# Normalising and turning one attention operand closer to its use, and a reordered first attention, in a two-layer fp32 attention kernel

## The chip, the cores and the metric

The kernel runs on one core of a Trainium2 chip. The metric is device time in microseconds (us). Three runs of the kernel before took 230.91, 231.04 and 232.44 us; the median is 231.04 us.

A core has five engines that follow queues of their own: TensorE (PE, matrix products and transposes, with a separate queue of weight loads, PEld), VectorE (DVE), ScalarE (ACT), GpSimd (POOL) and SyncE (SP, which here only issues transfers). They wait for each other by semaphores.

## The reference

There are two inputs, `x` and `ctx` (called c in the kernel), each 32 batches of 256 tokens by 256 features, fp32. Two layers follow each other.

```python
# L0: attention of x on ctx with 16 heads of 16 features
q, k, v = heads(x @ Wq.T), heads(ctx @ Wk.T), heads(ctx @ Wv.T)
att = softmax(q @ k.T / 4) @ v
x = x + att[0]                # batch 0's result is added to every batch

# L1
nX = layernorm(ctx) * norm1_w + norm1_b
nF = layernorm(x)   * norm2_w + norm2_b
attended = softmax(nF @ nX.T / 16) @ nX                   # each batch by itself
h = gelu(attended @ fc1_w.T + fc1_b)                      # 4 features
cross = h @ fc2_w.T + fc2_b
nC = layernorm(cross) * norm3_w + norm3_b
own = softmax(nC @ nC.T / 16) @ nC
out = nF + gamma2 * (cross + gamma1 * own)
```

Because only `att[0]` is used, L0 is worked out for batch 0 alone. Because `h` has four features, everything behind `attended` is done in a space of five to nine columns.

## The kernel before, in words

**Layout.** Batches go in quads (`QB = 4`, `NQ = 8` quads). The 256 tokens of a batch lie in two halves of 128 partitions. c has four rotating quad buffers, `cq`; x lies whole in `x_all`. Both are normalised in place, without the weights of the norm, which are folded into later operations.

**Order.** The program is written out by hand: the order of the calls is the order of the instructions in each engine's queue, and only the semaphores between engines are put in by the framework. So an instruction that waits holds up all that the code issues later on the same engine.

**The heads of L0** (L670 to L736). The 16 heads go in four groups of four. For each group, `head_queries` makes scores on PE, from which `head_maxima` takes the row maxima on DVE; `head_less` turns the maxima and subtracts them; `head_keys` makes the scores once more, the other way round, with ACT taking the exponential; `head_values` weighs the values with them, and `head_turned` turns the result into a part of `att`, which is complete after the fourth group. `project_values` makes the values that `head_values` needs. Between these calls stand the first steps for c: `stats(n)` (DVE, two `bn_stats` per batch), `moments_c` (POOL), `even_normed` (POOL normalises a batch's first 128 tokens) and `odd_normed` (ACT normalises the other 128). The small set-ups of weights (`setup_bias` and others) are spread among them.

**Between the heads and the steps** (L831 to L849) `add_attention` starts to add `att` to x: a transfer issued by POOL that adds `att`, broadcast over four batches (1 MB), into `x_all`. The first batches of x get it from DVE instead, by `add_first`.

**The loop** calls `first_step(s)` (L869) for s = 0, 1, ... A step makes the scores of batch s (`cross_scores`: eight matmuls `sc`, L779), then the maximum of each row (`nm`, DVE, L789), and the exponential (`e`, ACT, L792). Two steps later `cross_turned` turns the exponentials (PE, `pt_e`) and ACT copies them (`eTq`). By quad, `values` and `values_turned` make the reduced values of c, `cross_values` and `cross_weighted` the weighted sums. What makes later batches ready stands ahead of the scores in a step:

- `load_c(q)` and `load_x` are issued by SP. A load of c waits until its buffer is free, which is when the last batch of the quad four earlier has been turned and used.
- `stats_c` and `stats_x` put the statistics of a batch (`st`, DVE, L211) into tiles of a quad.
- `moments` (L213 to L241, on POOL unless another engine is given) turns the statistics of 8 or 16 columns into a factor `rs` and a shift `nmr`; it holds a power, `rs` from `ve` (L227). `moments_both(q)` does it in one block of 16 columns for the x of quad q and the c of quad q + 1, `moments_c` and `moments_x` for one alone.
- `norm_c` normalises both halves of a batch of c on POOL (L307). `norm_x` has POOL do one half (L329) and ACT the other (L331).
- `turn_c` turns a normalised batch of c (four transposes on PE, `pt_c`), which DVE or ACT copies to `nxT`; `turn_x` does the same for x with ACT (`nfT`, L761).
- Eight memsets (`zeroed`), six of them 128 x 1024, fill on POOL, in steps 8 to 15, tiles that the second part needs.

In the kernel before, in the steady part of the loop, step s takes the statistics of batch s + 12 of c, normalises batch s + 8 and turns batch s + 4. x keeps a distance of 8, 4 and 1. The last step of a quad calls the moments after its statistics:

```python
        if b == QB - 1 and 4 <= q + 2 < NQ:
            if q + 3 < NQ:
                moments_both(q + 2)
            else:
                moments_x(q + 2, 0, QB)
        if QB < s < B - 1:
            turn_x(s + 1)
```

After the loop the second part (the layer norm of `cross`, the attention of `nC` on itself, the output) follows in a written order; the change leaves it as it is.

Of the kernel before, what the change touches and what calls it, by code (L numbers as in the profile page):

```python
# [17 lines left out]
NC = D // P  # L18
# [4 lines left out]
QB = 4  # L23
# [4 lines left out]
def tile_xattn_seq(  # L28
# [179 lines left out]
    def statistics(st, src):  # L208

        for t in range(NC):  # L210
            nc.vector.bn_stats(st[:, t, :], src[:, t, :])  # L211

    def moments(st, n, name, eng=None):  # L213

        eng = eng or nc.gpsimd

        def t(what, c=1, bufs=2):
            return small.tile([P, n, c], F32, tag=f"{what}{n}", name=f"{what}_{name}", bufs=bufs)

        sm, df, sq, v4, ve, nm = t("sm", 2), t("df"), t("sq"), t("v4"), t("ve"), t("nmean")  # L220
        rs, nmr = t("rs", 1, 3), t("nmr", 1, 3)
        eng.tensor_sub(df, st[:, :, 1:2], st[:, :, 4:5])
# [4 lines left out]
        nc.gpsimd.tensor_tensor(  # L227
            rs.rearrange("p n o -> p (n o)"),
            ve.rearrange("p n o -> p (n o)"),
            neg_half[:, 0:n],  # L230
            ALU.pow,
        )

        def product():
            eng.tensor_scalar(nm, sm[:, :, 0:1], -0.5, 0.0, ALU.mult, ALU.add)
            eng.tensor_mul(nmr, nm, rs)  # L236
# [10 lines left out]
    def st_tile(q):  # L247

        if q not in st_of:
            st_of[q] = small.tile([P, 2, QB, NC, 6], F32, tag="st", name=f"st_{q}", bufs=5)  # L250
        return st_of[q]

    def stats_c(n):
        q, b = n // QB, n % QB
        statistics(st_tile(q - 1)[:, 0, b], cq_of[q][:, b])

    def stats_x(n):
        q, b = n // QB, n % QB
# [2 lines left out]
    def flat(st):  # L261
        return st.rearrange("p b t c -> p (b t) c")

    def moments_c(q):
        rn = moments(flat(st_of[q - 1][:, 0]), TQ, f"c{q}")
        for b in range(QB):
            mc_of[q * QB + b] = *rn, b * NC

    def moments_ahead(q):

        rs, nmr, product = moments(flat(st_of[q - 1][:, 0]), TQ, f"c{q}", nc.vector)
        for b in range(QB):
            mc_of[q * QB + b] = rs, nmr, b * NC
        return product

    def moments_x(q, lo, hi):
        rn = moments(flat(st_of[q][:, 1, lo:hi]), (hi - lo) * NC, f"x{q}_{lo}")
# [18 lines left out]
    def moments_both(q):  # L296

        rn = moments(st_of[q].rearrange("p k b t c -> p (k b t) c"), 2 * TQ, f"b{q}")
        for b in range(QB):
            mc_of[(q + 1) * QB + b] = *rn, b * NC  # L300
            mx_of[q * QB + b] = *rn, TQ + b * NC

    def norm_c(n):
# [361 lines left out]
    def stats(*ns):  # L665
        for n in ns:
            stats_c(n)
# [15 lines left out]
    less()  # L683
    head_maxima(1, sq, (1, 2, 3))
    setup_fc1()
    project_values(0, on_scalar)
    head_keys(0)
    setup_queries()
    stats(2)
    head_less(1)()  # L690
    setup_outer()
    stats(3)
    project_values(1, on_scalar)
    moments_c(0)
    even_normed(0, 1, 2, 3)
    sq = head_queries(2)
    stats(4)
    head_maxima(2, sq, (0, 1))
    head_values(0)
    setup_bias()  # L700
    head_maxima(2, sq, (2, 3))
    head_keys(1)
    odd_normed(0, 1)
    weighted = head_turned(0)
    stats(5)
    head_less(2)()
    weighted()
    sq = head_queries(3)
    stats(6)
    head_maxima(3, sq, range(QB))  # L710
    head_values(1)
    odd_normed(2, 3)
    head_keys(2)
    weighted = head_turned(1)
    stats(7)
    moments_c(1)
    even_normed(4, 5)
    head_less(3)()
    weighted()
    head_keys(3)  # L720
    stats(8, 9, 10)
    head_values(2, by_vector)
    stats(11)
    odd_normed(4)
    head_values(3, on_scalar, True)
    c_ends = moments_ahead(2)
    weighted = head_turned(2), head_turned(3)
    for f in weighted:
        f()
# [115 lines left out]
    ends()  # L845
    stats_x(2)
    ends = first_moments(2, 3)
    c_ends()
# [13 lines left out]
    ]  # L862


    scaled_at = [25, 26, 26, 27, 27, 28, 29, 29, 31, 31, 32, 32]

    first_ends = [ends]

    def first_step(s, between=()):  # L869
        q, b = s // QB, s % QB  # L870
        if b == 0 and 2 <= q and q + 4 < NQ:
            load_c(q + 4)
            if q == 2:
                load_x((NQ - 2) * QB, B)
        if s in (2, QB):
            add_attention((s // 2 + 2) * QB, (s // 2 + 3) * QB)
        elif b == 0 and 1 < q < NQ - 3:
            add_attention((q + 3) * QB, (q + 4) * QB)

        late_turn = s in (27, 29, 31)  # L880
        if 0 <= s - 2 < B and not late_turn:
            cross_turned(s - 2)
        if 2 <= s < 2 * QB:
            for n in (2 * s, 2 * s + 1):
                stats_x(n)
            if s < QB:
                ends = first_moments(2 * s, 2 * s + 2)
        if QB <= s and s + 3 * QB < B:
            stats_c(s + 3 * QB)
        if s >= 2 * QB and s + 2 * QB < B:  # L890
            stats_x(s + 2 * QB)
        if b == QB - 1 and 4 <= q + 2 < NQ:
            if q + 3 < NQ:
                moments_both(q + 2)
            else:
                moments_x(q + 2, 0, QB)
        if QB < s < B - 1:
            turn_x(s + 1)
        for n in {9: (12,), 10: (13, 14), 11: (15,)}.get(s, ()):
            norm_x(n)  # L900
        if 3 * QB <= s < B - 2 * QB:
            norm_x(s + QB)
        elif B - 2 * QB < s <= B - QB:
            norm_x(s + QB - 1)
        if s + QB < B and s >= QB:
            turn_c(s + QB, on_scalar if s < QB + 2 else by_vector)
        for n in {7: (13,), 8: (14, 15), 9: (16, 17), 10: (18,)}.get(s, ()):
            norm_c(n)
        if 2 * QB + 2 < s < B - 2 * QB:
            norm_c(s + 2 * QB)  # L910
        for n, at in enumerate(scaled_at):
            if s == at:
                scale_skip(n)
        if 2 * QB <= s < 2 * QB + len(zeroed):
            nc.gpsimd.memset(*zeroed[s - 2 * QB])
        if b == 2 and 1 < q < NQ:
            values_turned(q)
        if b == 1 and 1 < q < NQ:
            values(q)
        if b == 2 and 0 < q <= NQ:  # L920
            cross_values(q - 1)
        if b == 3 and 0 < q <= NQ:
            cross_weighted(q - 1)
        for f, *args in between:
            f(*args)
        if s < B:
            softmax = cross_scores(s)
            if s <= QB:
                turn_x(s + 1)
            if s == 0:  # L930
                turn_c(6, nc.scalar.copy)
            softmax()
        if late_turn:
            cross_turned(s - 2)
        if 1 <= s <= QB:
            stats_c(s + 3 * QB - 1)
        if s == 0:
            first_ends.pop()()
            add_first(3)
            first_ends.append(first_moments(3, QB))  # L940
            odd_normed(7)
        elif s == 1:
            first_ends.pop()()
            odd_normed(8)
            even_normed(8, 9)
        elif s == 2:
            ends()
            turn_c(7)
            load_c(5)
            odd_normed(9)  # L950
            even_normed(10)
        elif s == 3:
            ends()
            values(1)
            even_normed(11)
        elif s == QB:
            values_turned(1)
        if s in (QB, QB + 1):
            odd_normed(s + 6)
        if s == QB:  # L960
            moments_x(2, 0, 2)
        elif s == QB + 1:
            norm_x(2 * QB)
# [12 lines left out]
    n_flat = n_all.rearrange("p g t b c -> p (g t b) c")  # L976
# [373 lines left out]
```

## Time and profile before

| what | value |
|---|---|
| median of three runs | 231.04 us |
| the profiled execution | 231.46 us |
| its span in the trace | 229.7 us |
| mean granted clock of TensorE | 0.978 |
| PE busy | 210.5 us, 92 % of the span |
| DVE busy | 171.3 us, 75 % |
| ACT busy | 146.7 us, 64 % |
| POOL busy | 173.8 us, 76 % |
| transfers, mean rate | 147 GB/s |

The span is the time between the first and the last instruction of the trace, and the profiled execution's own time is 1.8 us longer. A share of the span is a mean over stages: the stages have different limits, so a change in one is read from the busy times and the waits of that stage. In the lines of the trace an entry such as `cq<-cq,rs_b,nmr_b 128x256` means output, inputs and shape; the first number of a timeline's line is the time in us since the start of the span, the second the duration, and `x2` means that the line stands for two instructions in a row. A line of the waits names the waiting instruction and line, behind the arrow what ended the wait, then the total, the number and the longest of these waits in us.

### The profile page before, as it was taken

What the parts mean: (1) busy time and instruction counts of PE and PEld (TensorE: products, weight loads), DVE (VectorE), ACT (ScalarE), POOL (GpSimd) and SP (SyncE); (2) the same over time, 40 slices, a digit from 0 to 9 for tenths busy, and PEclk for the clock granted to TensorE, in tenths of its full rate; (3) what the DMA queues carried; (4) which work ended last, traced back from release to release, by engine and by line L of the source; (5) the groups of instructions that cost most, each with busy time, mean ns of one, the idle gap of its engine ahead of it and who ended that gap; (6) DMA issues with size and microseconds to landing.
All of it is one profiled execution on the core that took longest, in us unless ns stands there. A gap on an engine that the chain in (4) does not pass through costs nothing.

```text
span 229.7 us, 4945 instructions
## 1 busy us (share of the span) xinstructions
PE 210.5 (92%) x1797; PEld 153.1 (67%) x1797; DVE 171.3 (75%) x408; ACT 146.7 (64%) x302; POOL 173.8 (76%) x274
## 2 busy tenths in 40 slices
PE   7999898898999989999999999989998979999950
PEld 6766555676787768697897887866675544665530
DVE  2797989899988748667686786777284994796991
ACT  2554968688988285966789967447847735636310
POOL 6067588576989999999979899996089999994000
PEclk9999999999999999999999999999999997999995
DMA  7899997999959974190730000000000002444596
GB/s 224 280 345 344 394 380 152 198 244 246 207 100 335 279 122 172 31 155 2 129 56 1 3 0 0 3 3 4 4 0 3 0 0 107 182 173 182 195 382 251
DMA packets 18038, 33.81 MB, mean 147 GB/s; under 512 B 1175, under 2 KB 2142, under 8 KB 18014
## 3 DMA queue, kind: packets, MB, share of 16 engines
q1 hardware_dynamic: 12974, 24.33, 30.1%
q0 software_dynamic: 3696, 7.34, 18.3%
q10 hardware_dynamic: 1344, 1.84, 2.3%
q8 instruction: 14, 0.23, 0.4%
q14 instruction: 10, 0.08, 0.1%
HBM read 17.73 MB, written 8.39 MB: 114 GB/s over the span
## 4 chain that ended last, share of the span: by engine, by line
PE 59%; DVE 15%; POOL 15%; ACT 6%; issue 3%; DVEq 1%; POOLq 0%; ACTq 0%
PE sc L779 15%; PE o L445 5%; PE pt_x L202 3%; PE pt_c L202 3%; PE pu L357 3%; PE pt_e L202 3%; DVE st L211 3%; POOL cq L307 3%; POOL rs_b L227 3%; PE k L445 3%; PE sc L445 2%; PE pv L357 2%; PE q L445 2%; POOL rs_x L227 2%; PE ph L357 2%
## 5 line engine op out<-in xcount | busy, mean ns | idle before, releaser
L779 PE MATMUL sc<-nxT,nfT 128*128 128x256 f32 x256 | 62.4, 386 | 0.7 <-ACT nfT L761 0.7
L779 PEld LDWEIGHTS sc<-nxT,nfT 128*128 128x128 f32 x256 | 45.7, 190 | 12.1 <-issue 5.3
L770 POOL TENSOR_TENSOR x_all<-x_all,w_bc 128x512 f32<-128x512 f32 x32 | 39.7, 1269 | 0.0
L789 DVE TENSOR_REDUCE nm<-sc 128x2 f32<-128x512 f32 x32 | 22.0, 688 | 22.8 <-PE sc L779 11.1
L792 ACT ACTIVATE e<-sc,nm 128x256 f32<-128x256 f32 x64 | 26.8, 472 | 19.0 <-DVE nm L789 18.8
L761 ACT ACTIVATE nfT<-pt_x,bq,wq 128x256 f32<-128x256 f32 x64 | 33.2, 581 | 1.6 <-PE pt_x L202 1.3
L211 DVE BATCH_NORM_STATS2 st<-x_all 128x6 f32<-128x256 f32 x64 | 23.2, 415 | 0.6 <-DMA x_all<-att 0.5
L1207 DVE TENSOR_TENSOR x_all<-o,x_all 128x1024 f32<-128x1024 f32 (+1 forms) x20 | 19.2, 1006 | 5.6 <-PE k L445 3.5
L202 PE MATMUL pt_x<-ident,x_all 128*128 128x128 f32 x132 | 20.4, 276 | 1.5 <-POOL x_all L329 1.3
L202 PE MATMUL pt_c<-ident,cq 128*128 128x128 f32 x132 | 19.7, 276 | 1.5 <-ACT nfT L761 1.0
L211 DVE BATCH_NORM_STATS2 st<-cq 128x6 f32<-128x256 f32 x56 | 20.6, 414 | 0.0
L202 PE MATMUL pt_e<-ident,e 128*128 128x128 f32 x128 | 19.5, 275 | 1.2 <-ACT eTq L801 0.7
L1202 ACT ACTIVATE eT<-k 128x512 f32<-128x512 f32 (+1 forms) x19 | 14.2, 798 | 8.5 <-PE k L445 8.4
L307 POOL TENSOR_SCALAR cq<-cq,rs_b,nmr_b 128x256 f32<-128x256 f32 x32 | 19.3, 676 | 0.0
L202 PEld LDWEIGHTS pt_e<-ident,e 128*128 128x128 f32 x128 | 15.4, 141 | 5.0 <-ACT e L792 1.5
L801 ACT COPY eTq<-pt_e 128x512 f32<-128x512 f32 x32 | 18.4, 587 | 0.3 <-PE pt_e L202 0.3
L202 PEld LDWEIGHTS pt_x<-ident,x_all 128*128 128x128 f32 x132 | 15.2, 141 | 4.6 <-POOL x_all L329 2.4
L345 DVE COPY nxT<-pt_c 128x512 f32<-128x512 f32 x23 | 15.6, 680 | 2.3 <-PE pt_c L202 2.2
L202 PEld LDWEIGHTS pt_c<-ident,cq 128*128 128x128 f32 x132 | 15.0, 141 | 3.0 <-ACT nfT L761 1.7
L331 ACT ACTIVATE x_all<-x_all,nmr_b,rs_b 128x256 f32<-128x256 f32 x16 | 9.8, 618 | 10.8 <-POOL nmr_b L236 10.8
L445 PE MATMUL o<-w_out,vt 32*128 32x256 f32 x128 | 14.7, 413 | 1.2 <-ACT eT L1202 0.6
L227 POOL TENSOR_TENSOR rs_x<-ve_x,neg_half 128x2 f32<-128x2 f32 (+2 forms) x9 | 9.4, 1043 | 4.1 <-DVE ve_x L226 3.1
(220 smaller groups left out, 438.9 us busy)
## 6 DMA issues: line engine op xcount, KB each, us to landing
out_dram<-x_all SPq DMA_DIRECT2D x16, 512.0 KB
x_all<-att POOLq DMA_DIRECT2D x7, 1024.0 KB, 9.3
cq<-in_ctx_dram SPq DMA_DIRECT2D x6, 1024.0 KB
x_all<-in_x_dram SPq DMA_DIRECT2D x4, 1024.0 KB
x_all<-in_x_dram SPq DMA_DIRECT2D x1, 2048.0 KB
x_all<-in_x_dram SPq DMA_DIRECT2D x1, 1792.0 KB
cq<-in_ctx_dram ACTq DMA_DIRECT2D x1, 1024.0 KB
cq<-in_ctx_dram SPq DMA_DIRECT2D x1, 768.0 KB
```

What stands on the lines that cost most here:

```text
L202: nc.tensor.transpose(pt[:, dc, t * P : (t + 1) * P], src[:, t, dc * P : (dc + 1) * P], ident)
L211: nc.vector.bn_stats(st[:, t, :], src[:, t, :])
L227: nc.gpsimd.tensor_tensor(rs.rearrange("p n o -> p (n o)"), ve.rearrange("p n o -> p (n o)"), neg_half[:, 0:n], ALU.pow,)
L307: nc.gpsimd.tensor_scalar(row, row, rs[:, i + t, :], nmr[:, i + t, :], ALU.mult, ALU.add)
L445: nc.tensor.matmul(dst[i][:, t, :], lhs[r : r + SL, t * P : (t + 1) * P], rhs[r : r + SL, :], start=True, stop=True,)
L761: nc.scalar.activation(nfT_of[n][:, dc, :], px[:, dc, :], AF.Identity, bias=bq[:, dc : dc + 1], scale=wq2[:, dc : dc + 1],)
L770: nc.gpsimd.tensor_mul(x_all[:, n], x_all[:, n], w2_bc.unsqueeze(1).to_broadcast([P, NC, D]))
L779: nc.tensor.matmul(sc[:, qt, :], nfT[:, dc, qt * P : (qt + 1) * P], nxT[:, dc, :], start=(dc == 0), stop=(dc == NC - 1),)
L789: nc.vector.tensor_reduce(nm, sc, AX.X, ALU.max, negate=True)
L792: nc.scalar.activation(e[:, qt, :], sc[:, qt, :], AF.Exp, bias=nm[:, qt : qt + 1])
L801: nc.scalar.copy(eT_of[q][:, b], turned(e_of.pop(n), "et", f"e_{n}"))
L1207: nc.vector.tensor_add(xs, po, xs)
```

## The change

Six things are changed at once.

1. c's distances in the loop. For quads 3 to 5 statistics are taken 8 steps ahead (12 before), the norm is done 4 ahead (8) and the turn 2 ahead (4). For quads 6 and 7 statistics stay 12 ahead; the norms are 6 ahead in quad 6 and 8 ahead in quad 7, the turns 4 ahead. Batches 8 to 11, quad 2, are turned 2 ahead.
2. The moments. `moments_both(q)` now joins c and x of the same quad (quads 3, 4 and 5, in steps 7, 11 and 15). c of quad 2 gets its own block on POOL in step 3, in place of the block that was worked out on DVE in the heads (`moments_ahead`, removed); its halves are normalised in steps 4 to 7. c of quad 6 gets a block in step 15, and c of quad 7 one in step 19, behind that of x of quad 6.
3. `values(q)` moves from the second to the fourth step of a quad, and `values_turned` from the third step to the first of the next quad, for quads 2 to 5.
4. At step 8 SP issues the last 2 MB of x ahead of the sixth quad's load of c, not behind it.
5. The eight memsets are issued by DVE, not POOL.
6. In the heads, `head_queries` and `head_keys` of a group stand ahead of `project_values` and `head_values`; statistics of quad 2 leave the heads for steps 0 to 3; two projections' copies change engine.

```diff
     def stats_c(n):
         q, b = n // QB, n % QB
-        statistics(st_tile(q - 1)[:, 0, b], cq_of[q][:, b])
+        statistics(st_tile(q)[:, 0, b], cq_of[q][:, b])
...
-    project_values(0, on_scalar)
     head_keys(0)
+    stats(2)
+    project_values(0, by_vector)
+    head_less(1)()
+    sq = head_queries(2)
+    stats(3)
     setup_queries()
-    stats(2)
-    head_less(1)()
+    project_values(1, on_scalar)
     setup_outer()
-    stats(3)
-    project_values(1, on_scalar)
     moments_c(0)
     even_normed(0, 1, 2, 3)
-    sq = head_queries(2)
+    head_maxima(2, sq, (0, 1))
+    head_keys(1)
+    head_maxima(2, sq, (2, 3))
+    less = head_less(2)
+    head_values(0)
+    less()
     stats(4)
-    head_maxima(2, sq, (0, 1))
-    head_values(0)
+    sq = head_queries(3)
     setup_bias()
-    head_maxima(2, sq, (2, 3))
-    head_keys(1)
-    odd_normed(0, 1)
+    stats(5)
+    odd_normed(0, 1, 2, 3)
+    head_maxima(3, sq, range(QB))
     weighted = head_turned(0)
-    stats(5)
-    head_less(2)()
+    head_keys(2)
+    head_less(3)()
     weighted()
-    sq = head_queries(3)
     stats(6)
-    head_maxima(3, sq, range(QB))
-    head_values(1)
-    odd_normed(2, 3)
-    head_keys(2)
-    weighted = head_turned(1)
+    head_keys(3)
     stats(7)
     moments_c(1)
     even_normed(4, 5)
-    head_less(3)()
+    head_values(1, by_vector)
+    head_values(2, by_vector)
+    weighted = head_turned(1)
     weighted()
-    head_keys(3)
-    stats(8, 9, 10)
-    head_values(2, by_vector)
-    stats(11)
     odd_normed(4)
     head_values(3, on_scalar, True)
-    c_ends = moments_ahead(2)
...
+    def at_steps(*lags):
+        at = {}
+        for lo, hi, lag in lags:
+            for n in range(lo, hi):
+                at.setdefault(n - lag, []).append(n)
+        return at
+
+    stats_at = at_steps((12, 24, 8), (24, 32, 12))
+    normed_at = at_steps((12, 24, 4), (24, 28, 6), (28, 32, 8))
+    turned_at = at_steps((8, 24, 2), (24, 32, 4))
...
         if b == 0 and 2 <= q and q + 4 < NQ:
-            load_c(q + 4)
             if q == 2:
                 load_x((NQ - 2) * QB, B)
+            load_c(q + 4)
...
-        if QB <= s and s + 3 * QB < B:
-            stats_c(s + 3 * QB)
+        for n in stats_at.get(s, ()):
+            stats_c(n)
         if s >= 2 * QB and s + 2 * QB < B:
             stats_x(s + 2 * QB)
-        if b == QB - 1 and 4 <= q + 2 < NQ:
-            if q + 3 < NQ:
+        if b == QB - 1 and 3 <= q + 2 < NQ:
+            if q + 2 < NQ - 2:
                 moments_both(q + 2)
             else:
                 moments_x(q + 2, 0, QB)
+            if NQ - 2 <= q + 3 < NQ:
+                moments_c(q + 3)
         if QB < s < B - 1:
             turn_x(s + 1)
-        for n in {9: (12,), 10: (13, 14), 11: (15,)}.get(s, ()):
-            norm_x(n)
-        if 3 * QB <= s < B - 2 * QB:
+        if 2 * QB <= s < B - 2 * QB:
             norm_x(s + QB)
         elif B - 2 * QB < s <= B - QB:
             norm_x(s + QB - 1)
-        if s + QB < B and s >= QB:
-            turn_c(s + QB, on_scalar if s < QB + 2 else by_vector)
-        for n in {7: (13,), 8: (14, 15), 9: (16, 17), 10: (18,)}.get(s, ()):
+        for n in turned_at.get(s, ()):
+            turn_c(n, on_scalar if n < 10 else by_vector)
+        for n in normed_at.get(s, ()):
             norm_c(n)
-        if 2 * QB + 2 < s < B - 2 * QB:
-            norm_c(s + 2 * QB)
...
-            nc.gpsimd.memset(*zeroed[s - 2 * QB])
-        if b == 2 and 1 < q < NQ:
+            nc.vector.memset(*zeroed[s - 2 * QB])
+        if b == 2 and NQ - 2 <= q < NQ:
             values_turned(q)
-        if b == 1 and 1 < q < NQ:
+        elif b == 0 and 2 < q < NQ - 1:
+            values_turned(q - 1)
+        if b == 1 and NQ - 2 <= q < NQ or b == 3 and 1 < q < NQ - 2:
             values(q)
...
-        if 1 <= s <= QB:
-            stats_c(s + 3 * QB - 1)
+        if s < QB:
+            stats_c(s + 2 * QB)
...
         elif s == 1:
             first_ends.pop()()
-            odd_normed(8)
-            even_normed(8, 9)
...
         elif s == 3:
             ends()
             values(1)
-            even_normed(11)
+            moments_c(2)
         elif s == QB:
             values_turned(1)
-        if s in (QB, QB + 1):
-            odd_normed(s + 6)
+            odd_normed(8)
+            even_normed(8, 9)
+        if QB < s < 2 * QB:
+            odd_normed(s + 4)
+        if QB < s < QB + 3:
+            even_normed(s + 5)
...
             norm_x(2 * QB + 1)
-            moments_c(3)
             norm_x(2 * QB + 2)
-            norm_c(3 * QB)
         elif s == QB + 3:
             norm_x(2 * QB + 3)
-        elif s == 2 * QB:
-            moments_both(3)
```

More of the change, by code (lines that the diff above doesn't have):

```diff
@@ L264, in moments_c @@
     def moments_c(q):
-        rn = moments(flat(st_of[q - 1][:, 0]), TQ, f"c{q}")
+        rn = moments(flat(st_of[q][:, 0]), TQ, f"c{q}")
         for b in range(QB):
             mc_of[q * QB + b] = *rn, b * NC
[L269 to L274, printed above, removed]
     def moments_x(q, lo, hi):
@@ L299, in moments_both @@
         for b in range(QB):
-            mc_of[(q + 1) * QB + b] = *rn, b * NC
+            mc_of[q * QB + b] = *rn, b * NC
             mx_of[q * QB + b] = *rn, TQ + b * NC
@@ L847, in tile_xattn_seq @@
     ends = first_moments(2, 3)
-    c_ends()
     values_turned(0)
@@ L949, in first_step @@
             load_c(5)
-            odd_normed(9)
-            even_normed(10)
         elif s == 3:
```

## The prediction

> **What bounds the kernel now.** I read the busy times in stretches first, then the waits, then the queues of GpSimd (POOL), VectorE (DVE) and TensorE (PE) around one block of moments. "Step s" is `first_step(s)`; times are of the profiled execution of the kernel before.
>
> ```profile
> core 0: us, PE busy (x) PEld busy (x) DVE busy (x) ACT busy (x) POOL busy (x), PEclk, DMA share, GB/s
> 4.86:34.17 29.31, 27.93 (x273) 18.29 (x272) 24.89 (x65) 18.22 (x41) 15.79 (x39) 1.00 1.00 349
> 34.17:58.41 24.24, 21.37 (x151) 16.03 (x150) 22.14 (x86) 20.10 (x44) 17.32 (x24) 1.00 0.95 211
> 58.41:97.00 38.59, 36.81 (x276) 28.75 (x276) 29.81 (x77) 28.28 (x64) 36.71 (x74) 1.00 0.69 177
> 97.00:141.35 44.35, 44.07 (x334) 36.71 (x330) 32.51 (x75) 34.34 (x74) 41.29 (x73) 1.00 0.28 47
> ```
>
> Up to 34 us (the heads of the first attention) PE and DVE alternate; to 58 us (steps 0 to 4) DVE is full; from step 5 on PE is. From 97 to 141 us (steps 14 to 25) PE is idle for 0.3 us of 44. So whatever makes PE wait in steps 5 to 25 is paid in full. POOL has 2 to 3 us of room there in each of the last two stretches.
>
> ```profile
> ACT x_all L331 <- POOL nmr_b L236: 10.8, 4, 5.1
> ```
>
> ScalarE (ACT) waits four times for the moments that POOL computes; the longest are 5.1 us (until 81.01) and 3.0 us (until 92.43). One block of them on POOL, that of step 19:
>
> ```profile
> 113.75 1.33 POOL L307 TENSOR_SCALAR cq<-cq,rs_b,nmr_b 128x256 f32<-128x256 f32 x2
> 116.30 0.23 POOL L222 TENSOR_TENSOR df_b<-st 128x16 f32<-128x16 f32 x1 [1.22 <-DVE st L211]
> ...
> 117.58 2.93 POOL L227 TENSOR_TENSOR rs_b<-ve_b,neg_half 128x16 f32<-128x16 f32 x1
> ...
> 120.99 0.55 POOL L329 TENSOR_SCALAR x_all<-x_all,rs_b,nmr_b 128x256 f32<-128x256 f32 x1
> 121.53 1.09 POOL L307 TENSOR_SCALAR cq<-cq,rs_b,nmr_b 128x256 f32<-128x256 f32 x2
> ```
>
> The block takes 4.7 us (116.30 to 120.99), 2.93 of them the power. It cannot start before DVE has the last statistics of the step, and those stand behind the step's previous maximum:
>
> ```profile
> 114.21 0.69 DVE L789 TENSOR_REDUCE nm<-sc 128x2 f32<-128x512 f32 x1 [1.43 <-ACT x_all L331]
> 114.82 0.74 DVE L211 BATCH_NORM_STATS2 st<-cq 128x6 f32<-128x256 f32 x2
> 115.48 0.73 DVE L211 BATCH_NORM_STATS2 st<-x_all 128x6 f32<-128x256 f32 x2
> ```
>
> Meanwhile PE goes on; a step is 3.05 us:
>
> ```profile
> 115.48 1.89 PE L779 MATMUL sc<-nxT,nfT 128*128 128x256 f32 x8
> 117.21 0.60 PE L202 MATMUL pt_e<-ident,e 128*128 128x128 f32 x4
> 117.65 0.60 PE L202 MATMUL pt_x<-ident,x_all 128*128 128x128 f32 x4
> 118.08 0.60 PE L202 MATMUL pt_c<-ident,cq 128*128 128x128 f32 x4
> 118.52 1.89 PE L779 MATMUL sc<-nxT,nfT 128*128 128x256 f32 x8
> ```
>
> Start to start, a turn (four transposes) is 0.44, scores 1.73, `values` or `cross_values` 1.00, a small turn 0.22. The kernel before survives the block because a batch of c is normalised 8 steps ahead and turned 4 ahead: four steps, over 12 us, lie between.
>
> **What the Trainium skill says.** "TensorE: Matmul & The Clock Gate", section "Architectural detail": ACT and DVE take their instructions strictly in order, GpSimd too. The trace agrees: behind the wait of 5.1 us the exponentials of batch 9, whose maximum was ready at 77.8, start at 81.52. "VectorE: DVE Perf Modes", section "Zero memsets can be issued as uint32": a memset takes one cycle per element. At the page's 0.96 GHz 256 elements are 0.267 us, and the trace's 128x256 memset on DVE took 0.272. The first page, Part 1, says that PE falls to half its clock after about 3.4 us without work; the trace has a granted clock of 0.59 and 0.56 in 192 to 196 us, after a thinly filled stretch.
>
> **The change, part by part.**
>
> *Heads.* DVE loses eight statistics of quad 2 (8 x 0.33 = 2.6) and five small operations (0.6), and gains two copies from ACT (0.4 each). PE issues scores ahead of projections, so the third head's scores start at about 17.0 instead of 18.48. I walked the queues with the durations of before. It comes back: `fc1b_all` on DVE now waits for `setup_bias` behind the fourth head's scores on PE, so the fourth maxima start at 24.4 (24.65 before). And `stats(7)` now stands behind the fourth `head_less`, ready at 29.4 instead of 27.8; 3.4 us later (27.8 to 31.17 before) the moments of quad 1 are there, at 32.8; `odd_normed(4)` waits for them on ACT, and the copy `col_h3` behind it comes at 33.3 (32.70). I take +0.4 us on `att`, between -0.9 and +1.0. Step 2, where DVE waits 0.5 for a power on POOL, absorbs it.
>
> *Steps 0 to 8.* PE turns two batches of c fewer (0.88 us, owed until steps 20 and 21). Quad 2's moments (3.3 us, as 65.58 to 68.87) move into step 3 of POOL, and its four halves (0.55 each) from steps 1 to 3, where POOL was waiting anyway, to 4 to 6. POOL then runs without a gap from 57.4: moments c2 to 60.7, `add_attention`'s issue and two halves to 62.6, x's first moments to 65.4, x 8 at 66.5 (62.5 before). ACT waits for each of these, and takes the copies of turns 8 and 9 in steps 6 and 7, 4.1 us of work in a step of PE. Scores 8 start at 72.6 instead of 70.95.
>
> *Steps 8 to 15.* The moments of step 8 move to 7, and six memsets of 0.90 leave POOL: the two waits of ACT shrink to about 0.5. They had cost PE 1.7 (scores 10 to 11 4.96 us, where 3.27 is work) and 0.8 (13 to 14). DVE takes the memsets, by the page's rate 1.07 each, and in 12 to 15 a third pair of statistics (0.66): 4.3 us in steps 12 and 13, over PE's 3 to 4; it falls 1.2 us behind by step 15. By my walk scores 16 start 0.3 us earlier than before, with 0.88 owed; I take +0.3 for all up to here, between -2 and +2.
>
> *Step 15 to 17.* Now `norm_c(19)` stands behind two blocks of moments in step 15, and PE turns batch 19 two steps later. From the end of scores 14: maximum 0.7, three pairs of statistics 2.0, moments b5 4.7, moments c6 3.3, `norm_x(19)` 0.55, `norm_c(19)` 1.09, the turn 0.44: scores 17 start after 12.8. PE's own work up to there: step 15 1.31 + 1.00 + 0.22, scores 1.73, step 16 1.31 + 0.22 + 1.73, step 17 1.31 = 8.8. PE stands for 4.0 us, and with DVE's lag of 1.2 for 5.2. I take 4.9.
>
> *Step 11 to 13* in the same way: 0.7 + 1.3 + 4.9 + 0.55 + 1.09 + 0.44 = 9.0 against 4.26 + 3.26 + 1.31 = 8.8; 0.2, in the +0.3 above. *Step 19 to 21:* 0.7 + 1.3 + 3.3 (x6) + 3.3 (c7) + 0.55 + 1.09 + 1.09 (batch 25) + 0.44 = 11.8 against 4.26 + 3.70 + 1.75 = 9.7: 2.1, I take 2.0. Behind PE's waiting turn stand the scores, and behind these all of DVE and ACT; nothing after step 21 works faster than PE, so nothing wins it back. POOL's extra lag at step 22 (2.4 us) meets slack: x 29 is ready 1.7 us before its turn now, and POOL stands idle from 158.8 to 165.
>
> *Transfers.* The 2 MB of x move from 67.8 on SP's queue to right behind `load_c(5)` (49.9), beside two of `add_attention`'s transfers. Those landed 8.5 to 13.8 us after issue; POOL issues that for x 16 to 19 at 60.7 (57.86), so it lands between 69 and 74.5, and DVE needs it at 71.6: 0 to 2.9, taken as 0. `load_c(6)` and `load_c(7)` wait for turns that come two steps later and still have three steps before their statistics: 0.
>
> Sum: 0.3 + 4.9 + 2.0 = 7.2. The profiled execution took 231.46 (span 229.7), the median of the runs is 231.04; 231.04 + 7.2 = **238.2 us**.
>
> **Rivals.** (1) The stalls at their least (4.0 + 1.5) and the first half winning 2.0: +3.5, 234.5. For it: the 2.5 us that PE now loses in steps 10 to 14 are certain to be touched; against it: POOL's full queue in steps 3 to 8. (2) The half clock: a stall of 4.9 us covers an idle window; 3.4 us at half rate cost 1.7, and with x 16 late by 1.5 it is 241.4. (3) The other side: PE does not wait for batch 19, since the block starts early enough, and only the two waits that go remain: 231.04 - 2.5 = 228.5. It decides at the distance from the last statistics of step 15 to the turn: 9.9 us of POOL work must fit where PE has 6. I see nothing that lets these statistics come 4 us earlier, as they stand behind the maximum of batch 14. That the change does not do what it says I exclude: the order of POOL's and PE's instructions in the new program is as I used it.
>
> **How the numbers follow.** Forecast 0.62, rival 1 0.20, rival 2 0.09, rival 3 0.05, no change 0.04. A change of 1% (2.3 us) is about what a measurement of this kernel tells from none: faster 0.05, same 0.06 (a little of rival 1 with it), slower 0.89. The range goes from -2 + 4.0 + 1.5 = +3.5, a little under 234.5, to rival 2: 234 to 241.5.
>
> **What would show it.** Right: a wait of PE (or its weight load) for POOL's normalisation of cq, L300 in the new numbering, of 4 to 5 us ahead of the turn of batch 19 and 1 to 2 us at 23 and 25; scores 16 about where they were, scores 24 some 7 us later; ACT's wait of 5.1 gone. Wrong in part: `att` before 33.5, or scores 8 no later than 71. Wrong altogether: no PE idle time over 2 us between scores 14 and 24.

## The result, and the profile after

The changed kernel takes 245.15 us (median of five runs, 244.72 to 245.48), beside 231.04 us before: a ratio of 1.0592, with a 95% interval from 1.056 to 1.0623. Slower was forecast, but by 7 us and not by 14; the time lies above the range of 234 to 241.5 us that was given.

Busy times of the changed kernel in four stretches, cut at the same events as the four shown of before (`att` complete, step 4, scores 14, step 25):

```profile
core 0: us, PE busy (x) PEld busy (x) DVE busy (x) ACT busy (x) POOL busy (x), PEclk, DMA share, GB/s
4.86:38.51 33.65, 30.79 (x272) 19.19 (x271) 22.44 (x54) 17.74 (x39) 14.20 (x38) 0.90 0.86 313
38.51:62.17 23.66, 21.27 (x150) 15.88 (x149) 21.99 (x84) 18.86 (x41) 15.23 (x22) 1.00 0.98 199
62.17:100.76 38.59, 34.47 (x253) 27.23 (x251) 32.34 (x78) 28.68 (x64) 34.41 (x69) 1.00 0.66 170
100.76:156.60 55.84, 49.57 (x360) 39.82 (x356) 37.59 (x90) 35.83 (x77) 45.17 (x87) 0.94 0.23 45
```

The first stretch is 4.3 us longer and the last 11.5 us; the two between are equal within 0.6 us. In both of the longer ones PE's granted clock is below 1.00, which it was not before; in the last, PE is idle for 6.3 us (0.3 before). Of the waits, those of ACT for the joint moments are nearly gone, as forecast, and a new one of PE has come:

```profile
PE pt_c L202 <- POOL cq L300: 4.4, 3, 4.0
...
ACT x_all L324 <- POOL nmr_x L236: 2.4, 2, 1.9
...
ACT x_all L324 <- POOL nmr_b L236: 1.0, 2, 0.7
```

**The wait in step 17.** POOL in steps 15 and 16 of the changed kernel (start, duration, instruction):

```profile
106.14 0.24 POOL L222 TENSOR_TENSOR df_b<-st 128x16 f32<-128x16 f32 x1 [4.68 <-DVE st L211]
...
107.44 2.93 POOL L227 TENSOR_TENSOR rs_b<-ve_b,neg_half 128x16 f32<-128x16 f32 x1
...
112.02 1.66 POOL L227 TENSOR_TENSOR rs_c<-ve_c,neg_half 128x8 f32<-128x8 f32 x1
...
114.13 0.56 POOL L322 TENSOR_SCALAR x_all<-x_all,rs_b,nmr_b 128x256 f32<-128x256 f32 x1
114.68 1.10 POOL L300 TENSOR_SCALAR cq<-cq,rs_b,nmr_b 128x256 f32<-128x256 f32 x2
```

The two blocks take 8.0 us (106.14 to 114.13), and batch 19 of c is normalised behind them, although its own factors have been ready since step 11. PE meanwhile:

```profile
110.69 0.60 PE L202 MATMUL pt_x<-ident,x_all 128*128 128x128 f32 x4
115.30 1.44 PE L202 MATMUL pt_c<-ident,cq 128*128 128x128 f32 x4 [4.01 <-POOL cq L300]
116.53 3.62 PE L769 MATMUL sc<-nxT,nfT 128*128 128x256 f32 x8
119.94 0.82 PE L202 MATMUL pt_e<-ident,e 128*128 128x128 f32 x4
```

It stands for 4.01 us, and what follows runs at half rate: the turn takes 1.23 from start to start (0.44 at full rate), the scores 3.41 (1.73), the next turn 0.66 (0.44). That is 2.7 us on top of the wait.

**Where the 13.7 us of the span come from.** I took start times of `sq` and `sc` from PE's timeline. The first head scores start at 9.0 to 10.4 us from run to run, so stretches are counted from there. Scores n are the score products of step n. Columns E1, E3 and E7 are experiments told below.

| stretch, us | before | changed | E1 | E3 | E7 |
|---|---|---|---|---|---|
| first head scores at | 9.10 | 9.33 | 9.25 | 10.23 | 9.08 |
| to scores 0 (the heads) | 30.47 | 34.58 | 30.74 | 30.48 | 30.48 |
| scores 0 to 8 | 31.38 | 33.20 | 33.15 | 33.20 | 33.21 |
| scores 8 to 16 | 32.45 | 31.42 | 31.38 | 31.42 | 31.41 |
| scores 16 to 20 | 15.12 | 23.27 | 23.84 | 19.31 | 16.39 |
| scores 20 to 24 | 15.11 | 17.08 | 17.06 | 16.45 | 16.84 |
| scores 24 to 31 | 35.21 | 35.22 | 35.16 | 35.81 | 36.88 |
| scores 31 to the end | 60.86 | 59.30 | 59.22 | 59.20 | 59.01 |

The changed kernel loses 4.1 us in the heads, 1.8 in steps 0 to 7, 8.2 in steps 16 to 19 and 2.0 in steps 20 to 23; it wins 1.0 in steps 8 to 15. The 4.1 us of the heads are not all fixed: E2 and E5, told below, have the same heads, and there they take 33.49 and 33.37 us, 2.9 to 3.0 more than before. The 1.6 us at the end are not the change's: with one and the same code there the last row is 60.46 us in E9 and 59.21 in E8, 60.87 in B1 and 59.3 in B2, and in each pair PE's clock is halved for some 3 us between 191 and 202 us in the longer one alone. The kernel before has this half clock (192.6 to 195.8 us), the changed one has not.

### The profile page after: what moved, and what is told of

Its sections match the earlier page's. It is cut to its first block, busy times and chain, and to the rows that moved or that the text cites. A ratio compares the mean times of both kernels' runs of the same rounds, so it can differ in the third digit from the quotient of the medians.

```text
span 243.4 us, 4964 instructions
## 1 busy us (share of the span) xinstructions
PE 214.8 (88%) x1797; PEld 154.8 (64%) x1797; DVE 176.4 (72%) x411; ACT 146.8 (60%) x300; POOL 171.8 (71%) x281
## 4 chain that ended last, share of the span: by engine, by line
PE 35%; POOL 7%; DVE 6%; ACT 4%; issue 2%; DVEq 1%; POOLq 0%; ACTq 0%
PE sc L769 9%; PE o L438 4%; PE pu L350 3%; PE k L438 2%; PE sc L438 2%; PE pt_c L202 2%; PE q L438 2%; PE pt_e L202 2%; PE pt_x L202 2%; DVE nm L779 1%; POOL rs_c L227 1%; PE pv L350 1%; PE pf L350 1%; POOL rs_b L227 1%; DVE x_all L1204 1%
## 5 line engine op out<-in xcount | busy, mean ns | idle before, releaser
L769 PE MATMUL sc<-nxT,nfT 128*128 128x256 f32 x256 | 63.8, 393 | 0.8 <-ACT nfT L751 0.8
L769 PEld LDWEIGHTS sc<-nxT,nfT 128*128 128x128 f32 x256 | 46.8, 194 | 11.4 <-issue 3.6
L202 PE MATMUL pt_c<-ident,cq 128*128 128x128 f32 x132 | 20.9, 282 | 8.1 <-POOL cq L300 4.4
L211 DVE BATCH_NORM_STATS2 st<-cq 128x6 f32<-128x256 f32 x64 | 23.3, 412 | 0.5 <-DMA cq<-in_ctx_dram 0.5
L300 POOL TENSOR_SCALAR cq<-cq,rs_b,nmr_b 128x256 f32<-128x256 f32 x24 | 16.3, 822 | 0.0
L438 PE MATMUL o<-w_out,vt 32*128 32x256 f32 x128 | 14.0, 401 | 1.2 <-ACT eT L1199 0.5
L324 ACT ACTIVATE x_all<-x_all,nmr_x,rs_x 128x256 f32<-128x256 f32 x20 | 11.9, 610 | 4.0 <-POOL nmr_x L236 2.4
L227 POOL TENSOR_TENSOR rs_x<-ve_x,neg_half 128x2 f32<-128x2 f32 (+2 forms) x10 | 10.6, 1060 | 5.0 <-DVE ve_x L226 4.7
```

Source lines behind the costliest of these rows:

```text
L202: nc.tensor.transpose(pt[:, dc, t * P : (t + 1) * P], src[:, t, dc * P : (dc + 1) * P], ident)
L300: nc.gpsimd.tensor_scalar(row, row, rs[:, i + t, :], nmr[:, i + t, :], ALU.mult, ALU.add)
L438: nc.tensor.matmul(dst[i][:, t, :], lhs[r : r + SL, t * P : (t + 1) * P], rhs[r : r + SL, :], start=True, stop=True,)
L769: nc.tensor.matmul(sc[:, qt, :], nfT[:, dc, qt * P : (qt + 1) * P], nxT[:, dc, :], start=(dc == 0), stop=(dc == NC - 1),)
```

## The experiments

Two places were to be separated: the heads, and the order of moments and norms on POOL.

**E1, the heads' order of before.** The diff of the heads shown above is undone, but for the statistics and the moments of quad 2, which stay in the steps.

```diff
...
-    sq = head_queries(3)
     setup_bias()
-    stats(5)
-    odd_normed(0, 1, 2, 3)
-    head_maxima(3, sq, range(QB))
+    head_maxima(2, sq, (2, 3))
+    head_keys(1)
+    odd_normed(0, 1)
     weighted = head_turned(0)
-    head_keys(2)
-    head_less(3)()
+    stats(5)
+    head_less(2)()
     weighted()
+    sq = head_queries(3)
     stats(6)
-    head_keys(3)
+    head_maxima(3, sq, range(QB))
+    head_values(1)
+    odd_normed(2, 3)
+    head_keys(2)
+    weighted = head_turned(1)
...
```

> The changed kernel with the order of the heads of before (the statistics of quad 2 and its moments stay in the steps). Theory H: the new order of the heads alone makes the first scores of the loop late (43.9 us in the changed kernel, 39.6 before), and the loop behind carries that to the end. First scores at 39.6 to 40.0, granted clock 1.0 from 28 to 35 us (0.5 in the changed kernel), total 245.15 - 4.3 = 240.9 us. Rival A: steps 3 to 8 are held by POOL's queue of moments and norms, so an earlier first score is lost again there; scores 8 stay within 1.5 us of 77.1 and the total is 243.5 or more.

Measured: 240.91 us, ratio 1.0432 (1.0384 to 1.048). The heads take 30.74 us, the clock is 1.00 from 28 to 36 us, and the stretches behind are within 0.6 us of the changed kernel's, so the loop gives back none of it. The heads cost some 4 us by this pair, and 3.1 by the pair of E2 and E3.

**E2, norms ahead of moments.**

```diff
-        if b == QB - 1 and 3 <= q + 2 < NQ:
-            if q + 2 < NQ - 2:
-                moments_both(q + 2)
-            else:
-                moments_x(q + 2, 0, QB)
-            if NQ - 2 <= q + 3 < NQ:
-                moments_c(q + 3)
...
         for n in normed_at.get(s, ()):
             norm_c(n)
+        if b == QB - 1 and 3 <= q + 2 < NQ:
+            if q + 2 < NQ - 2:
+                moments_both(q + 2)
+            else:
+                moments_x(q + 2, 0, QB)
+            if NQ - 2 <= q + 3 < NQ:
+                moments_c(q + 3)
```

> The changed kernel; in the last step of a quad POOL normalises first and then does the moments, nothing else moved. Theory M: PE's wait of 4.0 us for batch 19 and the half clock behind it (1.7 us) come from the two blocks of moments that stand ahead of that norm. The wait at 19 goes; the moments now end 1.6 us later and batch 20, normalised in step 16, is late by 1 to 2 us instead; the waits of step 21 (2 us) shrink to about 1. Total 245.15 - 5 = 240, between 238 and 241.5. Rival B: POOL is simply full in steps 15 to 22 and the wait only moves to batch 20 or later at its whole length: total 244 or more.

Measured: 241.92 us, ratio 1.0486 (1.0432 to 1.054). The gain over the changed kernel is 3.2 us and not 5, and the time lies just above the 238 to 241.5 that I had given. Steps 16 to 19 take 19.33 us (23.27). The wait for batch 19 is gone, one of 2.3 us for batch 20 has come, longer than I expected, and PE's clock stays at full rate from 97 to 141 us.

**E3, both.** The edits of E1 and E2 together.

> Both edits: the heads' order of before, and norms ahead of the moments on POOL. If H and M are separate places on one path, their gains add: 245.15 - 4.3 - 5 = 236 us (234 to 237.5). If one lag hides the other (rival A or B), the sum is less: 239 or more. What is left over 231.0 is the price of the shorter distances themselves.

Measured: 238.81 us, ratio 1.0337 (1.027 to 1.0404). E1 won 4.2 and E2 3.2; together they win 6.3, a little less than the sum of 7.4 and between the two cases I had set against each other (234 to 237.5, or 239 and more). They are two places on one path whose gains nearly add, and what is left over before was more than I had summed. PE in E3:

```profile
113.42 0.33 PE L202 MATMUL pt_c<-ident,cq 128*128 128x128 f32 x1 [2.29 <-POOL cq L300]
```

**E7, the moments of quad 6's c later.** E3, and `moments_c(6)` behind the norms of step 17.

```diff
-            if NQ - 2 <= q + 3 < NQ:
+            if q + 3 == NQ - 1:
                 moments_c(q + 3)
+        if s == 4 * QB + 1:
+            moments_c(NQ - 2)
```

> The run with the heads of before and with norms ahead of moments (238.8 us), and the moments of quad 6's c in step 17 behind its norms, not in step 15 (3.3 us on POOL). Theory M: the 2.3 us that PE still waits for batch 20 there are these 3.3 us, so the wait goes and nothing takes its place, since batch 24 is normalised in step 18: total 236 to 237. Rival: PE then waits for batch 24 or 25 (turned in steps 20 and 21) for as long: 238.5.

Measured: 234.97 us, ratio 1.0188 (1.015 to 1.0226). Steps 16 to 19 fall from 19.31 to 16.39 us: the block of 3.3 us was the rest of the wait. What stays of the loss there is 1.3 us, and PE's timeline shows it in step 20, where two batches of c are turned behind one of x:

```profile
118.46 0.60 PE L202 MATMUL pt_c<-ident,cq 128*128 128x128 f32 x4
119.89 0.63 PE L202 MATMUL pt_c<-ident,cq 128*128 128x128 f32 x4 [0.83 <-POOL df_x L222]
```

Batch 24 had been normalised by 117.0 (its two halves on POOL start at 115.90), so POOL is not what the second turn waits for, though the line names it. The turns of x and c share two PSUM buffers (tag `tp`). The second turn of c starts 0.1 us after DVE's copy of the first has ended, while ACT's copy of the turn of x in front of both (`nfT`, from 119.76, 1.04 us) still runs:

```profile
119.11 0.68 DVE L338 COPY nxT<-pt_c 128x512 f32<-128x512 f32 x1
```

Step 21 has the same wait (0.88 us, there put down to DVE's copy `nxT`). So it is the buffer of c's first turn that seems to be waited for. This was read from the times, and a third buffer was not tried.

E7 is still 3.6 us longer than before in the span. By the table 1.8 of these lie in steps 0 to 7, 1.3 in steps 16 to 19, 1.7 in steps 20 to 23 and 1.7 behind scores 24; it wins 1.0 in steps 8 to 15 and 1.9 at the end. What holds it behind scores 24 was not looked for.

**E4, E8, E9: what in the heads.** E4 puts values of the second group back ahead of the third keys, their copy back on ACT, and the first group's turn behind the fourth `head_less`. E8 is E4 with the bias ahead of the fourth queries, E9 is E8 with the norm on ACT behind the fourth values' copy; the second block shows what each of these two adds.

```diff
     head_maxima(3, sq, range(QB))
-    weighted = head_turned(0)
+    head_values(1)
     head_keys(2)
     head_less(3)()
-    weighted()
+    weighted = head_turned(0)
     stats(6)
     head_keys(3)
+    weighted()
...
-    head_values(1, by_vector)
```

```diff
-    sq = head_queries(3)
     setup_bias()
+    sq = head_queries(3)
...
-    odd_normed(4)
     head_values(3, on_scalar, True)
+    odd_normed(4)
```

> The changed kernel with one call of the heads put back: the values of the second group stand ahead of the third group's keys, as work for PE while it waits there, and the turn of the first group behind the fourth maxima's turn. Theory H1: the 32 products of two groups of values behind the fourth keys (3.6 us at half clock) are what the path gained; with 16 of them earlier and PE busy, the clock stays up: first scores at 41 or sooner (43.9), total about 242. Rival H2: the late maxima of the fourth group (25.7 us, held by the bias on VectorE) set the time, and the values lie beside them: first scores at 43 or later.

> The changed kernel with the values of the second group ahead of the third keys (242.5 us by itself, first scores 41.25), and the bias ahead of the fourth queries, so that VectorE no longer waits for it in front of the fourth maxima (from 25.7 us). Theory H2: the late maxima are the rest of the heads' loss; fourth maxima from about 24.5, first scores at 40.0 to 40.4, total 241 to 241.5. Rival: the rest is elsewhere (the statistics that stand behind the fourth maxima); first scores stay at 41 or later.

> The changed kernel with three calls of the heads moved: values of the second group ahead of the third keys and the bias ahead of the fourth queries (as in the run before), and ScalarE's half of batch 4 behind the copy of the fourth group's values, not in front of it. Theory H3: what is left of the heads' loss is that copy, which stands behind a norm that waits 1.8 us for POOL's moments of quad 1 (PE waits 1.3 us for the copy). From the first head scores to the first scores of the loop 31.33 us become 30.0 to 30.5, no more than before (30.47); total 240.5 to 241.5. Rival: the fourth group's exponentials set this end, and the copy gains under 0.3 us.

Measured: E4 242.49 us, ratio 1.0502 (1.0436 to 1.0568); E8 242.05, 1.0487 (1.0447 to 1.0528); E9 241.33, 1.0425 (1.0374 to 1.0476). The totals of the three overlap; the heads' own length does not. It is 33.37 to 34.58 us in the three profiles with the heads as changed (the changed kernel, E2, E5), then 32.01, 31.33 and 30.23; with the heads of before it is 30.47 or 30.48 in six profiles of eight, and 30.74 and 30.86 in the others. So the values were 1.4 to 2.6 us, the bias 0.7 and the copy 1.1. The range of the first comes from the clock: the three profiles with the heads as changed differ by 1.2 us in what is the same code, and the half clock lasts 6.8 us in the longest of them and 3.4 in the other two. In E4, E8 and E9 PE's clock is not halved in the heads at all. First scores at 41.25 in E4 came just behind the 41 I had named, and well ahead of the rival's 43. My expectation for E8 named the time of the first scores (40.0 to 40.4); measured it was 41.67, which by that yardstick was the rival's. The run had begun its heads 1.1 us later than E4, and only the distance shows the gain. The lines for the copy, in E4, first ACT and then PE:

```profile
33.90 0.60 ACT L315 ACTIVATE cq<-cq,nmr_c,rs_c 128x256 f32<-128x256 f32 x1 [1.84 <-POOL nmr_c L236]
34.40 0.35 ACT L361 COPY col_h<-ph 128x256 f32<-128x256 f32 x1
```

```profile
34.81 0.44 PE L368 MATMUL pt_h<-ident,col_h 128*128 128x128 f32 x2 [1.28 <-ACT col_h L361]
```

**B1 and E5, the memsets.** B1 is the kernel before with this edit; E5 is the changed kernel with its reverse.

```diff
-            nc.gpsimd.memset(*zeroed[s - 2 * QB])
+            nc.vector.memset(*zeroed[s - 2 * QB])
```

> The kernel before with one change: the eight memsets of steps 8 to 15 are issued by VectorE, not GpSimd. Theory G: the two waits of ScalarE for moments (5.1 us until 81.01 and 3.0 us until 92.43) stand behind memsets on POOL (0.9 us each), and cost PE 2.5 us; with the memsets gone each wait shrinks by 1 to 2 us and the total falls by 1 to 2.5 us, to 228.5 to 230. Rival: the memsets (0.9 us each) hold back the row maxima on VectorE by as much: no change, or up to 1 us slower.

> The changed kernel with the memsets back on GpSimd. Theory G: in the changed kernel scores 8 to 14 win 2.4 us back against before (23.65 us from scores 8 to 14, 26.05 before), and the memsets off POOL are why; back on POOL they cost 2 to 4 us, total 247 to 249. Rival: the gain there comes from the moments being one step earlier (steps 7 and 11); total within 1 us of 245.

Measured: B1 230.02 us, ratio 0.9905 (0.9875 to 0.9935): steps 8 to 15 take 30.70 us (32.45). E5 243.59 us, ratio 1.0558 (1.0516 to 1.0601), an interval that overlaps that of the changed kernel: steps 8 to 15 take 31.46 us (31.42), ACT's waits for the joint moments come to 0.3 us with the memsets on POOL too, and PE waits 3.5 us for batch 19 instead of 4.0. The rival had said within 1 us of 245, which it misses by 0.4. So the memsets are worth 1.75 us in the kernel before and win nothing in steps 8 to 15 of the changed one; there the theory that named them fell. That its gain of 1.0 us comes from the moments being done in steps 7 and 11 is the candidate left, and was not tried alone in that kernel.

**B2 and B3, the kernel before with more of the change.** B2 is B1 with its first `moments_both` at the end of step 7, not 8; B3 also normalises batch 14 of c in step 7 (the second hunk).

```diff
             norm_x(2 * QB + 3)
-        elif s == 2 * QB:
             moments_both(3)
...
-        for n in {7: (13,), 8: (14, 15), 9: (16, 17), 10: (18,)}.get(s, ()):
+        for n in {7: (13, 14), 8: (15,), 9: (16, 17), 10: (18,)}.get(s, ()):
```

> The kernel before with the memsets on VectorE (0.990 of before) and its first joint block of moments at the end of step 7, not of step 8, as the changed kernel has it. ScalarE still waits 4.2 us for that block (until 81.5), because the issue of a transfer and four norm halves (3.7 us) stand ahead of it on POOL. Theory: one step earlier the wait falls to about 1 us and scores 8 to 16 take about 1 us less than 30.70: total 0.5 to 1.5 us under the run with the memsets alone, ratio 0.985. Rival: batches 14 and 15 of c, now normalised behind the block, are late for their turns in steps 10 and 11: no gain, or up to 1 us lost.

> The kernel before with memsets on VectorE and the joint block at the end of step 7 (scores 10 came 1.45 us late there, since batch 14 of c was normalised behind the block), and now batch 14 normalised in step 7, ahead of the block. Theory: that late turn goes and ScalarE's wait stays at 1 to 2 us: steps 8 to 16 in 29.7 to 30.4 us (30.70 with the memsets alone, 31.43 in the run before), total 228 to 229. Rival: the block is late by those 1.1 us and the wait of ScalarE returns: 30.7 or more, total 229 to 230.

Measured: B2 229.26 us, ratio 0.9906 (0.9872 to 0.994); B3 228.65 us, ratio 0.9906 (0.9872 to 0.994). Steps 8 to 15 take 31.43 and 29.97 us (30.70 in B1). ACT's wait for the moments, in B1, B2 and B3:

```profile
ACT x_all L331 <- POOL nmr_b L236: 6.7, 4, 4.2
```

```profile
ACT x_all L331 <- POOL nmr_b L236: 2.4, 4, 0.9
```

```profile
ACT x_all L331 <- POOL nmr_b L236: 4.6, 4, 2.0
```

In B2 the wait goes as meant, but batch 14, now behind the block, holds PE in step 10, and the stretch is longer than in B1: the rival's case. In B3 that is mended. All three take about 1 % less than the kernel before, and each interval ends below 1; the ratios don't tell the three apart.

**E10, half of quad 2's moments off POOL.** E7, with the small operations of that block on DVE and only the power on POOL.

```diff
...
-            moments_c(2)
+            rn2 = moments(flat(st_of[2][:, 0]), TQ, "c2", nc.vector)
+            for i in range(QB):
+                mc_of[2 * QB + i] = *rn2[:2], i * NC
+            c2_ends.append(rn2[2])
         elif s == QB:
             values_turned(1)
+            c2_ends.pop()()
```

> The run with the heads of before, norms ahead of moments and quad 6's moments in step 17 (235.0 us), and of quad 2's moments in step 3 only the power left on POOL, the small operations on VectorE. Theory P: the 1.8 us that steps 0 to 8 lose against before (33.2 us, 31.4) are that block's 3.3 us on POOL in front of batch 8's norm (PE waits 1.6 us for it in step 6). With 1.6 us of it gone steps 0 to 8 take 31.6 to 32.3 us and the total is 234. Rival: ScalarE's copies of turns 8 and 9 and its waits for x's moments hold these steps: 33 us as now.

Measured: scores 0 to 8 take 32.21 us (33.21), at the upper part of what the theory gave, and the wait for batch 8 falls from 1.62 to 0.94 us. The total, 235.37 us (ratio 1.0183, 1.0147 to 1.0219), is that of E7 (1.0188). In the profiles the heads begin 0.9 us later than in E7, scores 8 to 16 take 0.2 us and 24 to 31 0.9 us more; a half clock falls into that last stretch (160.6 to 163.5 us), and the end is 0.5 us shorter. The block on POOL is half of the loss of 1.8 us at least; mending it alone brought no gain in the total that could be measured.

## Why the prediction was right or wrong, point by point

Two steps of the prediction failed most. The walk through the queues of the heads gave +0.4 us, where +4.1 was measured: it overlooked that the new order leaves PE without work while it waits for maxima. And the half clock behind the wait of step 17 was kept out of the sum, where it cost 2.7 us in this profile. The wait itself was forecast, and E2 shows its cause.

- **Heads: wrong, and the largest miss.** The prediction took +0.4 us on `att` (from -0.9 to +1.0) by a walk through the queues; measured +4.1 (2.9 and 3.0 in E5 and E2). The third head's scores started at 18.10 us where the walk had 17.0, behind the first projection (0.97 us), which still stands ahead of them on PE, and the fourth maxima at 25.73 where it had 24.4. It named two of the three costs, the bias in front of the fourth maxima (0.7) and `odd_normed(4)` in front of the last copy (0.6 forecast, 1.1 measured). It missed the third: with `head_values(1)` moved behind `head_keys(3)`, PE had nothing to issue while it waited for maxima and their turn. PE in the changed kernel:

```profile
25.16 0.70 PE L438 MATMUL sk<-qmT,kT 32*128 32x256 f32 x4
26.56 1.69 PE L438 MATMUL sk<-qmT,kT 32*128 32x256 f32 x12 [0.69 <-DVE m_all L479]
28.26 0.69 PE L486 MATMUL pm<-ident,m_all 128*128 128x128 f32 x2
29.52 2.09 PE L438 MATMUL sk<-qmT,kT 32*128 32x256 f32 x16 [0.57 <-DVE qmT L491]
31.54 3.64 PE L350 MATMUL ph<-eT_h,v 128*32 128x256 f32 x32
```

  The third keys wait in their middle until DVE has read maxima out of the banks that they need; then the clock halves (whether the idle time alone did this is open), the fourth keys take 2.09 us (1.15 at full rate), and the 32 products of two groups of values, which had been apart, 3.64. ACT waits with the fourth exponentials for the first 16 of them, since the two buffers of `eT_h` are taken:

```profile
33.60 2.06 ACT L500 ACTIVATE eT_h<-sk 128x512 f32<-128x512 f32 x4 [3.59 <-PE ph L350]
```

  A third buffer was not tried. Nor did step 2 absorb a delay of `att`, as the prediction had it: scores 0 to 8 take 33.20 us in the changed kernel and 33.15 in E1.
- **Steps 0 to 8: right.** Without the heads' 0.4 the forecast was +1.3; measured +1.8, at the place named: POOL's queue behind quad 2's moments (PE waits 1.62 us in step 6 for batch 8).
- **Steps 8 to 16: right in sign, half in size, wrong in cause.** The walk had steps 8 to 15 win about 2.0 us; they won 1.0. The waits of ACT did shrink, but the changed kernel does not owe that to the memsets. ACT's waits are as short in E5. One of the large memsets takes 0.91 us on DVE in the trace, where the prediction's estimate by the rate of the Trainium skill's page ("VectorE: DVE Perf Modes", section "Zero memsets can be issued as uint32") was 1.07; the measured time decides.
- **Steps 15 to 17: the mechanism right, the sum short, and one agreement luck.** The wait was put at 4.0 us, or 5.2 with DVE's lag, and 4.9 taken; measured 4.01. The lag was there: POOL's block begins 5.4 us after the start of scores 14 (100.76), where the prediction's terms give 4.4 (1.73 + 0.7 + 2.0). With the memsets on POOL (E5) it is 4.8. But PE turns the first half of batch 19 as soon as POOL has it, 0.5 us before the second half is ready, and its own work was some 0.4 us longer than the 8.8 taken. The two cancel the lag. What failed is that the half clock was left to a rival with a chance of 0.09 at 1.7 us: it came behind this wait in all six profiles that have the moments ahead of the norms, and cost 2.7 here. Its price for 3.4 us at half rate was nearly right (1.9 in E8, where it lasted so long).
- **Step 20: wrong.** The second turn was priced at its own 0.44 us; the wait for a buffer in front of it, told under E7, was left out. From the start of the first turn to the instruction behind the second it took 1.90, with 0.83 of waiting, where one turn takes 0.44. This makes up the stretch's 8.15: 4.01 + 2.69 + (1.90 - 0.44) = 8.16.
- **Steps 20 to 24: the sum nearly right, the mechanism not.** Forecast were 2.0 us for PE's wait for POOL's norm and 0.44 for the second turn; measured 2.0 for both. But PE hardly waits for POOL there (about 0.5 us for batch 23). In front of the turn of batch 25 it waits for DVE's copy, as in step 20:

```profile
134.56 0.33 PE L202 MATMUL pt_c<-ident,cq 128*128 128x128 f32 x1
135.09 0.55 PE L202 MATMUL pt_c<-ident,cq 128*128 128x128 f32 x3 [0.21 <-POOL cq L300]
136.52 0.63 PE L202 MATMUL pt_c<-ident,cq 128*128 128x128 f32 x4 [0.88 <-DVE nxT L338]
```

  That PE was already 1.5 us later from step 20 covers most of the wait that was forecast; that the sums agree is luck.
- **Transfers: right.** DVE waits 0.33 us for a transfer of x in step 16, while PE has work; of the rest none shows on the path.
- **The end: not forecast.** It was 1.6 us shorter, by a half clock that the same code has in one run and not in another.
- **The other side** (no wait at batch 19, 228.5 us) did not come. What it counted on, 2.5 us from ACT's two waits, is real as far as it was measured in the kernel before: 1.75 us with the memsets moved alone.

The miss in the span, 6.5 us (13.7 against 7.2), in the prediction's terms: heads +3.7, wait and half clock of step 17 together +1.8 over 4.9, the second turn of step 20 +1.0 over its own 0.44, steps 0 to 15 +1.5 (0.8 against -0.7), steps 20 to 23 -0.5, the end -1.6. The remaining 0.6 are what the prediction had taken off its walk (0.3: it took +0.3 up to step 15, where the walk gave -0.3 and 0.88 owed), where the run's heads began (0.2), and rounding.

## What to carry to other kernels

On an in-order engine a distance of so many steps is worth only what lies ahead of the instruction in its queue: count the blocks between an operand's readiness and the place where it is issued, and issue what is already computable ahead of the block (E2, E7). When products are deferred, ask whether they were the filler of a wait: moved behind the last stage they come onto the path and leave the engine idle where they were. A long idle wait of PE is to be priced with what may follow at half rate (here 1.8 to 3.3 us behind waits of 3.5 to 4.0, nothing behind 2.3). Small gains are to be measured from an event inside the run, not from its start, which lay 9.0 to 10.4 us ahead of the first head scores here.

## What the runs showed of the hardware

The half clock came in stretches of two lengths, both near a multiple of 3.4 us. By windows of 1 us it lasted in the changed kernel from about 28.2 to 35.1 and from 113.6 to 120.4 us, 6.8 each. Behind the same wait of step 17 it lasted 6.8 us in E1 and E4 too (waits of 3.99 and 3.98 us), but 3.4 in E8 and E9 (3.98 and 4.00) and in E5 (3.45). So the length of the wait does not tell which of the two comes. A wait of 2.29 us (E3) brought none. The heads of the changed kernel, 6.8 us at half clock, have 3.4 in E2 and E5. The Trainium skill, "TensorE: Matmul & The Clock Gate", Part 1, speaks of an activity window of about 3.4 us; these lengths agree with one such window and with two. But PE need not be idle for a whole window: ahead of the half clock at 192 us that the prediction names, in the kernel before, it was busy for 8.3 of 10 us (182 to 192). The two stretches of the changed kernel, then the first of them in E4 (window, its length, PE's busy time and instructions, granted clock, DMA share, GB/s):

```profile
28.00:36.00 8.00, 7.15 (x58) 0.57 0.99 364
113.00:121.00 8.00, 5.64 (x20) 0.57 0.48 82
```

```profile
28.00:36.00 8.00, 6.10 (x67) 1.00 1.03 378
```

From 25 to 28 us, ahead of the first, PE was busy for 2.3 us of 3 by the records (no gap over 0.7 us), and the clock fell; E4 kept the full clock at 6.1 of 8, and from 33 to 36 us at 1.7 of 3. Which measure of activity decides is open.
